# A convolution-attention hybrid on one core: two spreads of small vectors over channels go by way of DRAM instead of TensorE transposes

## The chip, the core and the metric

The kernel runs on 1 of the 8 cores of one Trainium2 chip. The metric is the device time of one execution in microseconds (us). The time before is 1663.79 us, the median of 3 runs (1658.05 to 1667.66). All profile figures come from one further execution that was recorded by the hardware profiler.

## What is computed

The input is four images of 32 channels, 128 x 128 float32. The reference has two layers; cut to what matters here:

```python
# layer 0: attention over channels' pixels, for each of 4 images b
q = pixel_unshuffle(x, 2).reshape(B, 128, 4096)        # 128 channels, 4096 positions
energy = einsum('bci,bcj->bij', q, q)                  # 4096 x 4096
d = sqrt(diagonal(energy))                             # norm of each position's vector
attn = softmax(energy / (d_i * d_j), axis=-1)
out = einsum('bcj,bij->bci', q, attn)
x = gamma * out + q                                    # back to image layout
# layer 1: tokens t = x as 8 x 8192 x 128
t = t + linear_attention(layernorm(t))                 # 8 heads
t = t + top2_of_8_experts(layernorm(t))
```

Two per-position vectors of layer 0 have to be multiplied into tiles whose rows are channels and whose columns are positions: `1/d` (the reciprocal norms, into the operand `qn` of the energy product), and `gamma / rowsum` (the reciprocal denominators of the softmax, into the attention output). Both vectors come about with positions on the partitions, because they are sums along the free dimension. So each must be turned and repeated over 64 rows ("spread") before the multiplication. The change concerns these two spreads alone.

## The kernel before

**Tiling.** The 4096 positions of an image are 8 chunks of 512 columns; one chunk is 4 blocks of 128. Only half of the symmetric energy matrix is computed. `attend` (L474) walks over chunk rows i = 0 to 7 and, in each, over jc = 0 to i: per 128 x 512 tile a matmul gives the energies (`pe`, L609), ScalarE takes the exponential (`pr`, L612), and a matmul adds its share to row i's output (`po`, L497). For jc < i the mirrored share is needed too: VectorE turns `pr` in 32 x 32 blocks into `F` (L421), `move` (L527) writes `F` to a DRAM tile `blocks` with one DMA (L530), and three steps later `bring` reads it back with the groups swapped in six DMAs (`swap_groups`, L545). These all go on SyncE's (SP's) queue. Some steps after that (`LAG = 57` units of an internal clock, L408) `transposed_share` (L429) uses `F` in four matmuls (`pg`, L433); VectorE then adds the result to `o[jc]` (L442). I call one passage of `F` through `blocks` a turn.

**Order.** The order of instructions on TensorE, VectorE, ScalarE and SP is the order in which the Python code issues them (`tc.manual_schedule`, L1413)[...]. Side jobs are generators. The list `timed` (L1414 on) has tuples (job, begin, end, count): the job is advanced by one `yield` whenever the image's progress, in per cent, asks for it, at a rate of count steps between begin and end. `steady` holds the closing work of each image (`layer1`), advanced once every `PACE = 10` clock units, and `stagger` (L166) passes each step on to several generators.

**First spread: `prep` (L348).** It prepares 2 chunks of an image (kc = 0 to 3; 16 calls in all with `prep_first`). It loads the pixels, turns them on VectorE into `qT`, squares and sums them (`squares`), and lets GpSimd (POOL) raise the sums to the power -1/2 (`pow_neg_half`, L163): `rn`, 128 x 8. VectorE then widens `rn` to `wide`, 128 x 4 x 2 x 64 (L388, two copies), four TensorE transposes against the identity put that into a PSUM bank `pnorm` (L399), and `scale` (L368) multiplies the pixels by it in four VectorE instructions (L372) into `qn`. `prep_first`, for the first two chunks, does this in another way (L344), which the change keeps.

**Second spread: `close_rows` (L731).** It closes two chunks of an image's output (kc = 0 to 3), once all mirrored shares are added (`missing()` is false). VectorE sums the denominators and takes reciprocals (L747, L748), widens them times gamma to `wide` (L752, two instructions), four TensorE transposes put that into a PSUM bank `pbd` (L774), and `divide` multiplies the output by it in four VectorE instructions (L761) into `df`. Then `df` is added to the tokens `T` (L783), their statistics follow, ScalarE normalises them (L696), and TensorE sums their Gram matrix (`pgram`, L728). For the last image `layer1` is split: the four `close_rows` run beside its attention, the rest after it (`last_parts`).

**Banks.** `hold` (L191) gives out one of three PSUM banks of the pool `ps_t` and makes sure that an earlier holder is emptied first; both spreads take a bank each time.

## Time and profile before

| quantity | value |
|---|---|
| time, median of 3 runs | 1663.79 us (1658.05 to 1667.66) |
| time of the profiled execution | 1659.2 us |
| its span, first to last instruction | 1657.4 us |
| mean granted clock of TensorE | 0.996 |
| TensorE (PE) busy | 1623.1 us, 98% of the span |
| VectorE (DVE) busy | 917.4 us, 55% |
| ScalarE (ACT) busy | 910.4 us, 55% |
| GpSimd (POOL) busy | 596.2 us, 36% |
| DMA | 332.81 MB in 241899 packets, mean 201 GB/s |

How to read it: a busy time is the union of an engine's instructions; TensorE's are pipelined, so one matmul's listed duration (mean ns) is longer than its slot in a row of matmuls, and the distance between two starts tells the slot. A float32 matmul of the program stands as two matmuls in the trace, a transpose as one. "Idle before" is the time in which an engine waited ahead of an instruction, with what ended the wait. SPq lines are the DMAs that SyncE's queue issues: their duration is the issue, not the transfer.

### The profile page before, as it was taken

The numbers are of one execution on the slowest core, as the hardware profiler recorded it, in microseconds if no ns is written. First come the engines' busy times: TensorE is split into PE (matmuls) and PEld (weight loads), VectorE is DVE, ScalarE is ACT, GpSimd is POOL, SyncE is SP. The second block draws the span as 40 slices with busy tenths as digits, with TensorE's granted clock in tenths as the row PEclk, the third lists the DMA queues.
The fourth block names the chain that finished last, engine by engine and source line by source line (L and its number), as shares of the span: only waits on it lengthen the run. The fifth ranks groups of instructions, "written<-read, shape, count | busy, mean of one in ns | idle before, by whom it ended". The sixth has DMA issues, their size and how long they took to land.

```text
span 1657.4 us, 21471 instructions
## 1 busy us (share of the span) xinstructions
PE 1623.1 (98%) x5288; PEld 856.9 (52%) x5288; DVE 917.4 (55%) x2359; ACT 910.4 (55%) x2863; POOL 596.2 (36%) x565
## 2 busy tenths in 40 slices
PE   8999999999999999999999999999999999999987
PEld 5444544455554455555564455555565445554643
DVE  4543353567486443559378453448559533344686
ACT  3555445566575555556575455556657455555376
POOL 1000000001014531456555543346546642436166
PEclk9999999999999999999999999999999999999999
DMA  4555656665349776986778868797668877885001
GB/s 147 199 181 174 198 186 213 230 212 170 131 171 277 246 220 213 271 249 176 207 200 254 265 208 255 214 287 200 167 196 239 277 222 246 240 254 168 15 14 39
DMA packets 241899, 332.81 MB, mean 201 GB/s; under 512 B 31984, under 2 KB 168304, under 8 KB 227440
## 3 DMA queue, kind: packets, MB, share of 16 engines
q1 hardware_dynamic: 207312, 291.92, 55.5%
q0 software_dynamic: 26624, 25.58, 7.5%
q10 hardware_dynamic: 7840, 13.93, 2.8%
q8 instruction: 45, 0.74, 0.2%
q14 instruction: 78, 0.64, 0.1%
HBM read 160.78 MB, written 175.80 MB: 203 GB/s over the span
## 4 chain that ended last, share of the span: by engine, by line
PE 84%; DMA 4%; DVE 4%; SPq 3%; ACT 2%; issue 2%; another core or an unknown queue 1%; POOL 0%; ACTq 0%; DVEq 0%; POOLq 0%
PE po L497 24%; PE pe L609 23%; PE pg L433 20%; PE pys L1117 3%; DMA blocks<-F 3%; PE py L1290 3%; PE pg L453 2%; SPq L545 2%; PE pat L854 2%; PE pys L1124 2%; PE pgram L728 1%; PE ptx L701 1%; DVE df L761 1%; PE pgv L839 0%
## 5 line engine op out<-in xcount | busy, mean ns | idle before, releaser
L612 ACT ACTIVATE pr<-pe 128x512 f32<-128x512 f32 (+1 forms) x576 | 322.4, 560 | 544.0 <-PE pe L609 448.2
L497 PE MATMUL po<-pr,qT 128*128 128x512 f32 (+3 forms) x1152 | 549.6, 559 | 4.2 <-ACT o L502 3.0
L609 PE MATMUL pe<-qn,qn 128*128 128x512 f32 x896 | 459.6, 595 | 2.6 <-ACT pr L612 1.6
L433 PE MATMUL pg<-F,qT 128*128 128x512 f32 x880 | 449.7, 592 | 1.1 <-DMA F<-blocks 1.1
L421 DVE STREAM_TRANSPOSE F<-pr 128x512 f32<-128x512 f32 x440 | 305.9, 702 | 144.8 <-ACT pr L612 127.0
L497 PEld LDWEIGHTS po<-pr,qT 128*128 128x128 f32 x1152 | 215.3, 190 | 251.7 <-issue 221.2
L1165 POOL DMA_INDIRECT acc<-ys,place x128 | 203.2, 1588 | 215.8 <-ACT pr L612 140.3
L438 ACT ACTIVATE junk<-F 128x512 bf16<-128x512 f32 x440 | 273.0, 620 | 1.2 <-DMA F<-blocks 1.2
L433 PEld LDWEIGHTS pg<-F,qT 128*128 128x128 f32 x880 | 166.7, 190 | 195.4 <-issue 181.0
L1053 POOL DMA_INDIRECT xs<-xn,place x192 | 186.0, 969 | 189.7 <-ACT pr L612 116.6
L609 PEld LDWEIGHTS pe<-qn,qn 128*128 128x128 f32 x896 | 155.0, 191 | 115.0 <-issue 104.6
L442 DVE TENSOR_TENSOR o<-o,pg 128x512 f32<-128x512 f32 x110 | 75.3, 684 | 207.9 <-PE pg L433 173.4
L1099 DVE TENSOR_TENSOR results<-pys,xn 128x256 f32<-128x256 f32 x120 | 49.9, 416 | 187.1 <-ACT xn L1093 122.0
L164 POOL TENSOR_TENSOR rn<-ss,neg_half 128x8 f32<-128x8 f32 (+1 forms) x17 | 27.2, 1602 | 320.9 <-DVE ss L296 320.8
L612 ACT ACTIVATION_READ_ACCUMULATOR pr<-pe 128x1 f32 x576 | 112.0, 194 | 0.0
L1093 ACT ACTIVATE xn<-pys 128x256 f32<-128x256 f32 x120 | 45.2, 377 | 112.5 <-PE pys L1124 94.5
L1117 PEld LDWEIGHTS pys<-ew_sb,xn 128*128 128x128 f32 x468 | 70.4, 191 | 53.0 <-issue 49.5
L1165 POOL DMA_INDIRECT yb<-ys,place x64 | 61.8, 965 | 84.5 <-DMA F<-blocks 31.1
L609 PE MATMUL pe<-qn 128*128 128x512 f32 (+3 forms) x256 | 90.2, 435 | 0.7 <-ACT qn L342 0.7
L438 ACT ACTIVATION_READ_ACCUMULATOR junk<-F 128x1 f32 x440 | 84.6, 192 | 0.0
L1117 PE MATMUL pys<-ew_sb,xn 128*128 x468 | 71.7, 275 | 0.4 <-ACT xn L1093 0.4
L164 POOL TENSOR_TENSOR rsa<-dm_a,neg_half 128x8 f32<-128x8 f32 x16 | 28.9, 1807 | 103.1 <-DVE sv_a L688 102.9
(216 smaller groups left out, 1521.1 us busy)
## 6 DMA issues: line engine op xcount, KB each, us to landing
blocks<-F SPq DMA_DIRECT2D x110, 1024.0 KB
F<-blocks SPq DMA_DIRECT2D x220, 192.0 KB
F<-blocks SPq DMA_DIRECT2D x220, 128.0 KB
xn<-xs SPq DMA_DIRECT2D x114, 132.0 KB
ys<-results SPq DMA_DIRECT2D x114, 128.0 KB
F<-blocks SPq DMA_DIRECT2D x220, 64.0 KB
below<-F SPq DMA_DIRECT2D x31, 384.0 KB
T<-in_x_dram SPq DMA_DIRECT2D x64, 128.0 KB
```

Of the source, the lines that this page charges most:

```text
L164: pinned(nc.gpsimd.tensor_tensor(dst, src, neg_half.to_broadcast(list(src.shape)), ALU.pow))
L421: f()
L433: nc.tensor.matmul(pg.rearrange("p (a f) -> p a f", a=4), st["qT"][i][:, ib, :], G[:, :, ib], start=(ib == 0), stop=(ib == NJ - 1),)
L438: nc.scalar.activation(junk, G[:, :, ib], AF.Copy, accum_out=st["sums"][:, NJ * i + ib, jc : jc + 1])
L442: nc.vector.tensor_tensor(st["o"][jc], st["o"][jc], pg, ALU.add)
L497: nc.tensor.matmul(row["po"][:, lo:hi], qT[blk // NJ][:, blk % NJ, :], w, start=start, stop=(row["left"] == 0))
L609: nc.tensor.matmul(pe[:, c0:], qn[jc][:, ts(j, P)], qn[i][:, c0:], start=True, stop=True)
L612: nc.scalar.activation(pr[:, c0:], pe[:, c0:], AF.Exp, accum_out=sums[:, t, i : i + 1]).ins
L1053: inst = nc.gpsimd.indirect_dma_start(xs[h], offset(place[:, i, k : k + 1]), xn[:, k, :], None)
L1099: nc.vector.tensor_tensor(result[:, :n], p[:, 2 * P : 2 * P + n * D].rearrange("p (j c) -> p j c", c=D), bufs[g % 6][:, :n, D : D + 1].to_ ...
L1117: nc.tensor.matmul(p[:, 2 * P + j * D : 2 * P + j * D + D], bufs[6 + g % 2][:, j, :D], weights[:, bass.ds(begins[2 * (g % 2) + j], D)], st ...
L1165: inst = nc.gpsimd.indirect_dma_start(to, None, ys, offset(place[:, i, k : k + 1]), compute_op=op)
```

## The change

In both spreads the widening on VectorE and the four transposes on TensorE go, for 14 of the 15 calls of `prep` (all but image 0, kc = 1) and for kc = 0, 1, 2 of `close_rows` in each image (kc = 3 stays as it was). In their place stands `spread_over_rows`:

- the vector is put into the first 8 columns of a 128 x 32 tile (`norms[0]` and `norms[1]` in turn for the norms, written by GpSimd directly; `norms[2]` for the denominators, times gamma in one VectorE instruction); the tiles are set to 1.0 once at the start;
- VectorE transposes it in 32 x 32 blocks into `turned`, so that each group of 32 partitions holds whole rows of positions;
- one step later SP writes `turned` to a DRAM tile of 128 x 32 (16 KB);
- five steps later SP reads it back in two DMAs, each to 64 partitions, every partition getting the same 4 pieces of 128 values (512 B); five steps later it is used.

The multiplications `scale` and `divide` read the result from SBUF, with another order of the columns (a, j, t for j, a, t), and are otherwise as before.

`close_rows` for kc < 3 now sums the denominators as soon as the image's last row of exponentials has passed its two chunks (`seen`) and the closing of kc - 2 has divided, ahead of the wait for the mirrored shares; after that wait it divides at once. It waits for kc - 1 to be added, and kc = 0 for the previous image's `sorted`, after the spread. `prep` for b + 1, kc = 3 is now advanced at 17 steps between 36% and 54% of the image (before: 38% to 62%), and the number of steps of a call of `prep` rises from 17 to 25 (image 0: from 16); what is left over runs on at the same rate. `place` has one buffer where it had two.

```diff
--- before.py
+++ after.py
@@ -318,6 +318,10 @@
                 xa[:, s, k].rearrange("p r (h t) e -> p (r h) e t", h=2),
             )
 
+    norms = [const.tile([P, S], F32, tag=f"norm{n}", name=f"norm_{n}") for n in range(3)]
+    for norm in norms:
+        nc.gpsimd.memset(norm, 1.0)
+
     def prep_first(st):
 
         b, kc = 0, 0
@@ -326,7 +330,7 @@
         qT = chunks_of(b, kc, st)
         yield
         ss = stat.tile([P, 2 * NJ], F32, tag="ss", name=f"ss_{b}_{kc}")
-        rn = stat.tile([P, 2 * NJ, 1], F32, tag="rn", name=f"rn_{b}_{kc}")
+        rn = norms[0][:, : 2 * NJ][:, :, None]
         for s in range(2):
             turn_quarters(s, xa, qT)
             squares(b, kc, s, qT, ss)
@@ -345,6 +349,25 @@
             done()
             yield
 
+    def spread_over_rows(norm, nm, tag, spread, gap):
+
+        turned = stat.tile([P, S], F32, tag="turned", name=f"turned_{nm}")
+        nc.vector.transpose(turned, norm)
+        yield
+        kept = dram.tile([P, S], F32, tag="norms", name=f"norms_{nm}", bufs=3)
+        nc.sync.dma_start(kept, turned)
+        for _ in range(gap):
+            yield
+        wide = work.tile([P, CH], F32, tag=tag, name=f"spread_{nm}", bufs=2)
+        for s in range(2):
+            nc.sync.dma_start(
+                wide[ts(s, 64)].rearrange("p (a f) -> p a f", a=4),
+                kept.rearrange("(a q) t -> a (q t)", q=S)[:, ts(s, P)].partition_broadcast(64),
+            )
+        spread.append(wide)
+        for _ in range(gap):
+            yield
+
     def prep(b, kc, st):
 
 
@@ -375,20 +398,27 @@
                     view(spread[own]),
                     ALU.mult,
                 )
-        rn = stat.tile([P, 2 * NJ, 1], F32, tag="rn", name=f"rn_{b}_{kc}")
+        on_chip = b == 0 and kc == 1
+        norm = norms[kc % 2]
         for s in range(2):
             squares(b, kc, s, qT, ss)
             if s == 1:
-                pow_neg_half(rn[:, :, 0], ss)
-            yield
-        for _ in range(ahead - 2):
-            yield
+                pow_neg_half(norm[:, : 2 * NJ], ss)
+            yield
+        if not on_chip:
+            yield from idle(1)
+            yield
+            spread = []
+            yield from spread_over_rows(norm, f"{b}_{kc}", "qs", spread, 5)
+            for s in range(2):
+                scale(s, spread[0], lambda ap: ap.rearrange("p (a j t) -> p a j t", a=4, t=S))
+            yield
+            return
+        rn = norm[:, : 2 * NJ][:, :, None]
         wide = work.tile([P, NJ, 2, 64], F32, tag="qs", name=f"wide_{b}_{kc}", bufs=2)
         for s in range(2):
             nc.vector.tensor_copy(wide[:, :, s], rn[:, ts(s, NJ)].to_broadcast([P, NJ, 64]))
         yield
-        if b:
-            yield
 
         def scale_all(bank):
             for s in range(2):
@@ -612,6 +642,8 @@
                         nc.scalar.activation(pr[:, c0:], pe[:, c0:], AF.Exp, accum_out=sums[:, t, i : i + 1]).ins
                     ]
                     own.append(pr)
+                    if i == NCH - 1 and j == NJ - 1:
+                        st.setdefault("seen", set()).add(jc)
                     if ending and jc == order[-1] and j == NJ - 1:
                         st["exps"] = True
                     after(2, partial(values, pr[:, c0:], t, c0, CH))
@@ -661,7 +693,7 @@
         lg = stat.tile([P, KT, E], F32, tag="lg", name=f"lg_{b}", bufs=1)
         first, second = (stat.tile([P, KT, E], F32, tag=nm, name=f"{nm}_{b}", bufs=1) for nm in ("first", "second"))
         weight = stat.tile([P, 2, KT, 1], F32, tag="weight", name=f"weight_{b}")
-        place = stat.tile([P, 2, KT], U32, tag="place", name=f"place_{b}")
+        place = stat.tile([P, 2, KT], U32, tag="place", name=f"place_{b}", bufs=1)
         begin = stat.tile([P, 2, NT + 1], U32, tag="begin", name=f"begin_{b}", bufs=1)
         turns = [[], []]
         gate = first
@@ -739,18 +771,31 @@
             late_rows = alone and kc >= 2
             last_rows = alone and kc == 3
 
-            while "exps" not in st if last_rows else missing():
-                yield from idle(1)
-            while b > 0 and kc == 0 and not states[b - 1].get("sorted"):
+            def summed():
+                return {2 * kc, 2 * kc + 1} <= st.get("seen", set()) and (kc < 2 or kc - 2 in st["divided"])
+
+            for flag in ("divided", "added"):
+                st.setdefault(flag, set())
+            far = kc < 3
+            while not summed() if far else "exps" not in st if last_rows else missing():
                 yield from idle(1)
             den, rd = (stat.tile([P, 2 * NJ], F32, tag=nm, name=f"{nm}_{b}_{kc}") for nm in ("den", "rd"))
             nc.vector.tensor_reduce(den, st["sums"][:, ts(kc, 2 * NJ), :], AX.X, ALU.add)
             nc.vector.reciprocal(rd, den)
-            wide = work.tile([P, NJ, 2, 64], F32, tag="grp", name=f"rdx_{b}_{kc}", bufs=2)
-            for s in range(2):
-                one = rd[:, ts(s, NJ)][:, :, None]
-                nc.vector.tensor_scalar(wide[:, :, s], one.to_broadcast([P, NJ, 64]), gam, None, ALU.mult)
+            if far:
+                norm = norms[2]
+                nc.vector.tensor_scalar(norm[:, : 2 * NJ], rd, gam, None, ALU.mult)
+                spread = []
+                yield from spread_over_rows(norm, f"den_{b}_{kc}", "grp", spread, 5)
+            else:
+                wide = work.tile([P, NJ, 2, 64], F32, tag="grp", name=f"rdx_{b}_{kc}", bufs=2)
+                for s in range(2):
+                    one = rd[:, ts(s, NJ)][:, :, None]
+                    nc.vector.tensor_scalar(wide[:, :, s], one.to_broadcast([P, NJ, 64]), gam, None, ALU.mult)
+            while far and missing() or not (kc - 1 in st["added"] if kc else b == 0 or states[b - 1].get("sorted")):
+                yield from idle(1)
             df = work.tile([P, 8, HW2, 2], F32, tag="df", name=f"df_{b}_{kc}", bufs=1)
+            spread_view = "p (a j t) -> p a j t" if far else "p (j a t) -> p a j t"
 
             def divide(pb):
                 for s in range(2):
@@ -761,26 +806,32 @@
                         nc.vector.tensor_tensor(
                             df[own].rearrange("p (a k) (h t) r -> p r a (k h) t", a=4, h=2)[:, r2],
                             o[rows].rearrange("p (a j t) -> p a j t", a=4, t=S),
-                            pb[own].rearrange("p (j a t) -> p a j t", a=4, t=S),
+                            pb[own].rearrange(spread_view, a=4, t=S),
                             ALU.mult,
                         )
 
-            yield
-            if not last_rows:
-                yield
-                yield
-            pb, done = hold(f"pbd_{b}_{kc}", divide)
-            for j in range(NJ):
-                nc.tensor.transpose(pb[:, ts(j, P)], wide[:, j].rearrange("p s c -> p (s c)"), ident)
-            yield
+            if not far:
+                yield
+                if not last_rows:
+                    yield
+                    yield
+                pb, done = hold(f"pbd_{b}_{kc}", divide)
+                for j in range(NJ):
+                    nc.tensor.transpose(pb[:, ts(j, P)], wide[:, j].rearrange("p s c -> p (s c)"), ident)
+                yield
             while missing():
                 yield from idle(1)
-            done()
+            if far:
+                divide(spread[0])
+            else:
+                done()
+            st["divided"].add(kc)
             if not late_rows:
                 yield
                 yield
             tk = T[:, ts(kc, 8), :]
             nc.vector.tensor_tensor(tk, tk, df.rearrange("p k w r -> p k (w r)"), ALU.add)
+            st["added"].add(kc)
             bs, stats = batch_stats("a", 8 * kc, 8)
             for j in range(8):
                 stats[j]()
@@ -1451,7 +1502,7 @@
         timed = []
         if b + 1 < B:
             timed.append((prep(b + 1, 2, nxt), 0.5, 16, 17))
-            timed.append((prep(b + 1, 3, nxt), 38, 62, 17))
+            timed.append((prep(b + 1, 3, nxt), 36, 54, 17))
     for steps, _ in steady:
         for _ in steps:
             pass
```

## The prediction

> **What bounds the kernel now.** I read the page's busy times and slices first, then the busy time by stage, then what TensorE waited for.
>
> ```profile
> PE 1623.1 (98%) x5288; PEld 856.9 (52%) x5288; DVE 917.4 (55%) x2359; ACT 910.4 (55%) x2863; POOL 596.2 (36%) x565
> ...
> PE   8999999999999999999999999999999999999987
> ...
> DMA  4555656665349776986778868797668877885001
> ```
>
> TensorE is at work everywhere but at the two ends; no other engine comes near. DMA engines are two thirds busy, more in the slices where experts' rows are moved. By stretches of 41 or 42 us (busy us of PE, PEld, DVE, ACT, POOL, then clock, DMA share, GB/s):
>
> ```profile
> 580.00:621.00 41.00, 41.00 (x149) 22.54 (x148) 17.64 (x32) 21.13 (x67) 16.52 (x19) 1.00 0.70 217
> ...
> 1326.00:1367.00 41.00, 39.41 (x126) 19.97 (x125) 13.13 (x27) 21.93 (x70) 19.67 (x22) 1.00 0.71 219
> ...
> 1492.00:1533.00 41.00, 37.58 (x117) 19.09 (x116) 19.13 (x45) 21.14 (x68) 27.50 (x29) 0.97 0.57 167
> 1533.00:1574.00 41.00, 37.35 (x197) 27.30 (x196) 27.99 (x90) 15.68 (x41) 6.25 (x7) 0.95 0.07 16
> ```
>
> Of 34.3 us of idle TensorE, 6.4 lie in the first 41 us and 20.0 after 1492 us; the 1450 us between have 7.9. There the time is the sum of TensorE's slots, and a slot taken out is a slot gained, unless a new wait fills it. TensorE's waits (total us, times, longest):
>
> ```profile
> PE pnorm L399 <- DVE wide L388: 2.8, 2, 2.5
> PE ptd L523 <- ACT gd L513: 2.4, 1, 2.4
> ...
> PE pg L433 <- DMA F<-blocks: 1.1, 1, 1.1
> ```
>
> The pnorm wait is nearly all that of image 0, kc = 1, which the change keeps. The mirrored shares waited once for a DMA.
>
> [...]here whole landings take longer (the chain shows 2.8 to 3.4 us for F<-blocks).
>
> **Removed.** Rows by form (count | busy us, mean ns | idle before):
>
> ```profile
> L752 DVE TENSOR_SCALAR rdx<-rd,gam 128x256 f32<-128x256 f32 x32 | 10.3, 364 | 0.6
> L774 PE MATMUL pbd<-ident,rdx 128*128 128x128 f32 x64 | 9.6, 273 | 0.1
> ...
> L399 PE MATMUL pnorm<-ident,wide 128*128 128x128 f32 x60 | 9.5, 283 | 2.8 <-DVE wide L388 2.8
> ...
> L388 DVE COPY wide<-rn 128x256 f32<-128x256 f32 x30 | 7.9, 304 | 1.1 <-POOL rn L164 1.1
> ```
>
> The slot of a set of four is seen in TensorE's timeline (start, us, what):
>
> ```profile
> 331.84 0.60 PE L774 MATMUL pbd<-ident,rdx 128*128 128x128 f32 x4
> 332.28 1.02 PE L609 MATMUL pe<-qn,qn 128*128 128x512 f32 x2
> ```
>
> From the set's first start to the next matmul's: 0.44 us. I looked at all 31 sets: 0.44 in 26 and 0.46 to 0.49 in 4 more, the first apart (0.78, with its wait). 56 pnorm transposes (14 sets) and 48 pbd transposes (12 sets) go: 26 x 0.44 = **11.4 us**, all on a TensorE without gaps. VectorE loses 28 x 0.304 + 24 x 0.364 = 17.2 us.
>
> **Added on engines.** VectorE gets 26 transposes of 128 x 32 and 12 small multiplications. A transpose of 128 x 128 takes 283 ns and of 128 x 256 412 ns in this trace, so about 0.19 us by the slope (estimate): 4.9 us, and 12 x 0.17 = 2.0. So VectorE has 10 us less. `scale` and `divide` stay the same: 682 to 687 ns with a PSUM operand, 681 ns for the sum of two SBUF tiles of 512 columns (L1200). VectorE is 45% idle: nothing on the path. Three memsets fall into POOL's wait from 2.2 to 8.4 us. Nothing: 0.
>
> **Added on SP and the DMAs.** 26 x 3 = 78 DMAs join some 1000 on SP. Six F<-blocks issue in 2.7 us, so a spread costs about 1.3 us of SP. Its 640 packets, at the 71 ns that a q1 packet takes now (55.5% of 16 engines x 1657 us over 207312), are 2.8 us of all 16 engines, 74 us in all: 4.5% more of a load of 66%. This matters only where `F` is late already. I paired each turn's six issues with its first pg matmul: of 141 turns the issue ends 5 to 28 us before use, mostly 10 to 17. Eleven have 7.5 us or less (rows 5 to 7 of the first image, row 2 of the last two, row 7 of the last). The tightest but one, in SP's timeline:
>
> ```profile
> 1495.89 6.61 SPq L545 DMA_DIRECT2D F<-blocks  x6
> 1502.60 0.37 SPq L530 DMA_DIRECT2D blocks<-F  x1
> ```
>
> and its use in TensorE's:
>
> ```profile
> 1507.52 1.02 PE L433 MATMUL pg<-F,qT 128*128 128x512 f32 x2
> ```
>
> The issue ends at 1502.5, use is at 1507.5, and landing takes 3 to 4 us: a margin of about 1. In the order of the built instructions some eight of these eleven have a spread's DMAs within the turns before them. Each pays from 0 to about 1.3 us (SP's time), so 0 to 10 us together. Below nothing is excluded here; the timing of `prep` 3 moves four pixel loads away from the token loads that crowd SP before 1326 us (1.6 us idle there), worth at most that. I take **+2.5 us**.
>
> **Moved.** The built order of TensorE is the same but for the removed sets, `pgram` groups some rows earlier, and the tail. `qn` is ready 19 or more matmuls ahead of its first use (in the tightest case, image 0's chunk 4: 42 before), some 16 us; no loss. The spreads of denominators start while `missing()` still holds. On the new waits: SP waits for VectorE's `turned` one step after its issue, with turns queued behind; VectorE waits for the spread five steps after the reads. A step of `close_rows` is 10 clock units of about 0.25 us (an image is 1568 units in some 388 us), so 12 us stand against a landing of 3 to 4 us; in `prep` more. POOL's power was waited for before too, at the same distance. Cost 0; without that cover see the slow rival.
>
> In the tail (last image), kc = 2 closes earlier, so more `pgram` and `ptx` lie before the last po instead of in the gaps after 1547 us. But o[6]'s sum waits in front of kc = 2's statistics on VectorE, and the last po now stands behind kc = 2's first pgram, which needs those statistics. Walking both orders through with the slots above, the last `divide` ends within 0.5 us of where it did without the stalls at 1526 to 1534 us, and PE's later part, with its 36 spare transposes of 5.0 us, begins up to 3 us sooner. Between -4 and +3; I take **-1**.
>
> **Sum.** -11.4 + 2.5 - 1 = -9.9 us on the profiled execution's 1659.2 us: 1649.3, a ratio of 0.9940. That execution stands 4.6 us under the median shown, so 1663.8 x 0.9940 = **1653.8 us**.
>
> **Rivals.**
> - *The late F eats the gain.* For it: margins of 1 us, and SP as the issuer of all turns. Against: a single DMA wait of 1.1 us today. At 8 to 10 us of waits and no gain in the tail, 1663.8 - 11.4 + 9 = about 1661.
> - *Slower: VectorE stands still at spreads.* VectorE waits in order for a read that sits in SP's queue behind blocked DMAs; behind it wait the block transposes for `F`, so later turns start late too. It decides from SP being over 8 us behind (12 us less 4 us of landing). Single waits of SP now reach 9.6 us ahead of a turn and 13.4 us ahead of the last stores, so it can be reached, but seldom. If it happened at 20 of 26 spreads, each holding TensorE by 1.1 us: +22 - 11.4 gives about 1674.
> - *More than the slots.* If the stalls of 4 us at 1526 to 1534 us go with the new order, 1653.8 - 5 gives about 1648.
> - That the transposes are not removed can't be: the built order lacks them. That another engine becomes the bound: VectorE and ScalarE are at 55%.
>
> **Chances.** Slots gained with little loss (1648 to 1659) 0.60; late F (about 1661) 0.27; more than the slots 0.06; slower 0.07. The range takes the first three with the bounds of F and tail: 1646 to 1665. A measurement can tell about 0.5% (8.3 us) from no change: under 1655.5 is faster. That has most of the first case and the third: 0.60; slower by over 0.5% is the slow case alone, 0.07; the rest, 0.33, within.
>
> **What would show it.** PE busy falls by 11 to 16 us (sets overlap in the union); PE's idle time between 41 and 1492 us stays under 12 us. PE's waits for F<-blocks show the loss: up to 4 us as predicted, 8 or more for the first rival. VectorE's waits for spread on its `scale` and `divide` rows should be near 0; tens of us there speak for the slow rival. The prediction is wrong if TensorE's idle time grows by more than 5 us in the middle, or if the tail after 1492 us changes by more than 4 us.

## The result and the profile after

| | before | after |
|---|---|---|
| median | 1663.91 us, 6 runs, 1658.05 to 1667.66 | **1683.88 us**, 6 runs, 1681.23 to 1691.76 |
| ratio, 95% interval | | **1.0132** (1.0102 to 1.0161) |
| profiled execution, its span | 1659.2, 1657.4 us | 1683.45, 1681.7 us |
| mean granted clock | 0.996 | 0.993 |
| PE idle between 41 and 1492 us | 7.5 us | 27.8 us |

The changed kernel is 1.3% slower; 0.6% faster was forecast. (Below, each experiment's ratio is to the kernel before in the same set of runs; in the third and fifth set that kernel ran at 1651 us and in the others at 1660 to 1664, for a reason that no profile here shows, so ratios of these two sets are not laid beside the others'.)

The page after, the engines' rows as shown of before:

```profile
PE 1624.8 (97%) x5184; PEld 849.0 (50%) x5184; DVE 908.5 (54%) x2345; ACT 912.3 (54%) x2863; POOL 599.2 (36%) x568
...
PE   8999999989999999999999999999999899998897
```

TensorE runs 104 instructions fewer (5288 to 5184), so the transposes are gone, and yet it is busy 1.7 us longer: what remained got slower. There are eights in the middle now, where there were none. The same four stretches by the clock (columns as before: busy us of PE, PEld, DVE, ACT, POOL, then clock, DMA share, GB/s):

```profile
580.00:621.00 41.00, 41.00 (x146) 22.23 (x145) 16.34 (x30) 21.37 (x66) 17.52 (x19) 1.00 0.79 239
1326.00:1367.00 41.00, 36.55 (x89) 16.46 (x88) 13.88 (x23) 17.81 (x57) 25.05 (x27) 0.96 0.70 214
1492.00:1533.00 41.00, 36.93 (x96) 16.61 (x94) 20.02 (x44) 18.86 (x60) 15.00 (x15) 0.99 0.83 245
1533.00:1574.00 41.00, 39.18 (x133) 21.83 (x133) 20.77 (x58) 21.97 (x69) 25.43 (x24) 0.93 0.36 91
```

The first is as full as before. The second has lost 2.9 us of TensorE's time and shows a clock of 0.96, with nothing of the tail in it yet. TensorE's waits (total us, times, longest):

```profile
PE pgram L760 <- ACT xn L728: 13.6, 7, 3.3
PE pys L1175 <- DMA xn<-xs: 7.0, 8, 2.0
PE pe L639 <- ACT pr L642: 6.2, 2, 4.4
PE pg L463 <- DMA F<-blocks: 4.8, 3, 2.7
```

The forecast looked for `F`, which is last here and near its size (4.8 us; up to 4 said). The first two rows are new. In the rows by form (count | busy us, mean ns | idle before) `pgram` was, before,

```profile
L728 PE MATMUL pgram<-xn 128*128 128x128 f32 x256 | 34.1, 277 | 0.5 <-ACT xn L696 0.5
```

and is, after, with the two multiplications that read the spreads:

```profile
L760 PE MATMUL pgram<-xn 128*128 128x128 f32 x256 | 42.8, 307 | 13.8 <-ACT xn L728 13.6
...
L806 DVE TENSOR_TENSOR df<-o,spread_den 64x512 f32<-64x512 f32 x48 | 32.9, 685 | 8.8 <-DMA ys<-results 5.7 <-DMA spread_den<-norms_den 2.2
L395 DVE TENSOR_TENSOR qn<-xx,spread 64x512 f32<-64x512 f32 x48 | 32.7, 682 | 13.1 <-DMA spread<-norms 12.6
```

256 Gram matmuls wait 13.8 us and take 8.7 us more. VectorE stands 12.6 us for the norms' spreads, but only 2.2 us for those of the denominators; `df` waits 5.7 us for something the forecast never named, a store `ys<-results`.

**Where the time comes in.** The 1152 `pe` matmuls of the attention are the same in all kernels, so the start of the k-th one is a milestone. Differences to before in the profiled execution, between milestones; "image's end" is from 24 `pe` matmuls ahead of it to 48 after it, where the closings stand:

| us against before | up to image 0's end | end 0 | end 1 | end 2 | `pe` 1008 to 1032 | `pe` 1130 on | all |
|---|---|---|---|---|---|---|---|
| after | -2.8 | +4.2 | +8.6 | +10.3 | +3.4 | +3.1 | +24.2 |
| `norms_timing` | -3.7 | -1.0 | -0.5 | -0.5 | -1.8 | +2.8 | -3.0 |
| `order_only` | -0.2 | +3.2 | +3.6 | +3.4 | -1.0 | -1.0 | +8.6 |
| `order_only_b` (the same kernel) | +0.8 | +3.3 | +6.8 | +3.4 | -0.8 | -2.2 | +13.6 |
| `order_dmas` | +1.4 | +4.7 | +8.8 | +8.5 | -3.1 | -0.7 | +19.7 |
| `dens_only` | +1.1 | +6.0 | +8.2 | +6.9 | -1.0 | +0.4 | +21.0 |
| `dens_later` | -0.1 | +6.4 | +3.0 | +2.5 | -0.7 | +6.7 | +16.7 |
| `divide_later` | -2.8 | +4.8 | +4.3 | +7.3 | +3.0 | +5.6 | +18.4 |
| `own_dens` | +0.4 | +6.0 | +3.5 | +2.3 | -2.4 | +0.1 | +9.1 |
| `own_after` | -1.7 | +4.9 | +5.1 | +6.7 | 0.0 | +1.7 | +16.6 |
| `own_after_kc1` | -1.3 | +4.0 | +1.8 | +1.8 | -3.1 | -1.8 | +5.2 |

(The rows are the experiments below; stretches left out make up the sum. Each row is one execution. Executions of the kernel before lie up to 8 us from their median, so a total is no sharper than that. A stretch is sharper, but not always: the two executions of one kernel, `order_only` and `order_only_b`, agree within 0.2 us at two ends and differ by 3.2 us at the third.) Between the ends, where nothing waits, the changed kernel gains what was forecast: from `pe` 400 to 552 it is 1.31 us ahead, three sets of 0.44. At each end of an image it loses 4 to 10 us.

### The profile page after: what moved, and what is told of

Read it like the earlier page. It is cut to its first block, busy times and chain, and to the rows that moved or that the text cites. A ratio compares the mean times of both kernels' runs of the same rounds, so it can differ in the third digit from the quotient of the medians.

```text
span 1681.7 us, 21331 instructions
## 1 busy us (share of the span) xinstructions
PE 1624.8 (97%) x5184; PEld 849.0 (50%) x5184; DVE 908.5 (54%) x2345; ACT 912.3 (54%) x2863; POOL 599.2 (36%) x568
## 4 chain that ended last, share of the span: by engine, by line
PE 81%; DMA 6%; DVE 5%; ACT 2%; issue 2%; SPq 2%; POOL 2%; another core or an unknown queue 0%; ACTq 0%; DVEq 0%; POOLq 0%
PE po L527 24%; PE pe L639 23%; PE pg L463 19%; PE pys L1168 3%; PE py L1341 3%; PE pg L483 2%; PE pgram L760 2%; DMA xn<-xs 2%; PE pat L905 2%; PE pys L1175 1%; DVE df L806 1%; POOL yb L1216 1%; DMA F<-blocks 1%; PE ptx L733 1%; SPq L575 1%
## 5 line engine op out<-in xcount | busy, mean ns | idle before, releaser
L164 POOL TENSOR_TENSOR norm<-ss,neg_half 128x8 f32<-128x8 f32 (+1 forms) x17 | 27.3, 1604 | 338.1 <-DVE ss L296 338.0
```

What stands on the lines that cost most here:

```text
L164: pinned(nc.gpsimd.tensor_tensor(dst, src, neg_half.to_broadcast(list(src.shape)), ALU.pow))
```

## The experiments

The theories that the expectations name with letters were these. A: VectorE, standing still at the norms' spreads, holds up what is queued behind it. B: the changed order of the closings brings TensorE to `pgram` before ScalarE's `xn` is there. C: the three DMAs of each spread make SP's queue, and with it other transfers, late. D came last and says which transfer: the stores `ys<-results`. An edit is shown against the changed kernel, if nothing else is said.

### One part alone

`norms_only` has the closings as they were, and `prep` as changed. `dens_only` has `prep` as it was, at 38 to 62%, and the closings as changed.

> The norms go through DRAM as in the changed kernel; the denominators are turned by TensorE as before. Theory A (the last steps of the next image's chunk 1 are all drawn at once at an image's end, so VectorE stands for the landing of its spread there): three waits of VectorE of 4 us on qn's rows stay, and most of the loss with them: 14 sets x 0.44 = 6 us gained, 12 to 15 us lost, so 1670 to 1674. Theory B (the closings' divide now comes four steps earlier before pgram's neighbours, and TensorE reaches pgram before ScalarE's xn): the loss goes with the denominators, so 1658 to 1661, TensorE's waits for xn back to 0.5 us. Theory C (SP's queue is late for everything behind a spread): loss in proportion to DMAs, 42 of 78, so about 1674.

> The denominators go through DRAM as in the changed kernel; the norms are turned by TensorE as before, and the timing of the preparation is the one before. Theory A: no wait of VectorE at the image's ends, so 12 sets x 0.44 = 5 us gained and little lost: 1659 to 1662. Theory B: TensorE's waits for xn (13.6 us in 7) stay, so 1670 to 1674. Theory C: in proportion to DMAs, 36 of 78, so about 1673.

Measured: `norms_only` 1661.37 us, ratio 0.999 (0.9977 to 1.0003); `dens_only` 1681.03, 1.0109 (1.0091 to 1.0128). The loss is, for the most part, in the denominators, and larger than any theory said for `dens_only` (1674 at most). `dens_only` has none of the norms' spreads, and has 15.1 us of `pgram` waits in 6: so A, if it costs anything, can't be the main cause. `norms_only` also has `place` with one buffer, so that part of the change is not the cause either.

### Giving the norms' steps time; dividing later

```diff
 prep_in_time:
-            timed.append((prep(b + 1, 1, nxt), 80, 99, 17))
+            timed.append((prep(b + 1, 1, nxt), 80, 99, 25))
 divide_later:
             if far:
+                for _ in range(4):
+                    yield
                 divide(spread[0])
```

> The changed kernel with one number changed: the next image's chunk 1 gets 25 steps in its stretch, as many as it has now, where it had 17. Theory A: VectorE's three waits of 4 us for the spread go (under 1 us left), the ends of images 0 to 2 give back 4 us each, so 1670 to 1673. Theory B: TensorE's waits for xn stay at 13 us, the time at 1681 to 1685. Theory C: SP is as late, 1681 to 1685.

> The changed kernel with four steps put back between the last share of a closing and its divide, as before. Theory B: TensorE's waits for xn fall from 13.6 us to under 3 us, so 1670 to 1674. Theory A and C: under 3 us of change, 1681 to 1685.

Measured: `prep_in_time` 1697.3 us, 1.0207 (1.0182 to 1.0232), `divide_later` 1681.25, 1.0124 (1.01 to 1.0148). The first missed badly: its VectorE still stood 14.4 us at `qn`, up to 9.4 us in one go, so more steps did not give the reads time, and image 0's end alone is 12.9 us longer than before, for 4.2. As a test of A it decides nothing; it shows that the number of steps isn't harmless. `divide_later` moved the waits more than the time. TensorE's waits of `pgram` for `xn` fell from 13.6 us in 7 to 3.4 in 1; none is left at the ends of images 0 to 2, and ends 1 and 2 cost 4.3 and 7.3 us for 8.6 and 10.3. But in the last image `pgram` waits 7.6 us for 5.8, 4.1 of them for `xnT`, and the stretch from `pe` 1130 on costs 5.6 us for 3.1; the median can't be told from the changed kernel's (the intervals overlap).

### The order without the transfers

`order_only` keeps the changed order of the closings, but spreads the denominators on TensorE as before, right ahead of the division, with eleven empty steps where the spread's steps were, and has the norms as before: no DMA is added. `order_only_b` is the same kernel once more.

```diff
             if far:
-                divide(spread[0])
-            else:
-                done()
+                pb, done = hold(f"pbd_{b}_{kc}", divide)
+                for j in range(NJ):
+                    nc.tensor.transpose(pb[:, ts(j, P)], wide[:, j].rearrange("p s c -> p (s c)"), ident)
+            done()
```

> Denominators turned by TensorE again and norms as before the change, no new DMA at all, but the closings keep the changed kernel's order: the same steps, the same conditions, pgram at the same places of TensorE's program (2 to 4 pe matmuls nearer to its statistics than before). Theory B (the new order of the closings lets TensorE reach pgram before ScalarE's xn): the loss stays, TensorE's waits for xn are 10 us or more and the time is 1676 to 1686. Theory C (the new DMAs make SP and the DMA engines late): nothing is added, so the time is that of before, 1661 to 1664.

> The same kernel as order_only, on this chip, to stand beside the other three: 1.004 to 1.006. If its ratio is 1.009 or more here, the ratio of these kernels to the one before depends on the chip, and only kernels of one call may be compared closely.

Measured: 1669.56 us, ratio **1.0048** (1.0032 to 1.0064), and 1669.96, 1.005 (1.0032 to 1.0069). No transfer is added and no transpose removed: the new order alone costs 8 us. That is less than theory B said (1676 to 1686, with waits for `xn` of 10 us or more; they are 5.1 us in 5), so the order is a part of the loss. The timeline (start, us, what) at the end of image 1, with SP's last store of the results and VectorE's first division ahead of TensorE's Gram matmuls, before:

```profile
735.61 0.39 SPq L1103 DMA_DIRECT2D ys<-results  x1
...
739.22 2.78 DVE L761 TENSOR_TENSOR df<-o,pbd 64x512 f32<-64x512 f32 x4 [0.48 <-PE pbd L774]
...
757.66 1.05 PE L728 MATMUL pgram<-xn 128*128 128x128 f32 x8
...
761.12 1.95 PE L728 MATMUL pgram<-xn 128*128 128x128 f32 x16
```

and in `order_only`:

```profile
739.44 0.39 SPq L1144 DMA_DIRECT2D ys<-results  x1
...
741.22 2.79 DVE L795 TENSOR_TENSOR df<-o,pbd 64x512 f32<-64x512 f32 x4 [1.07 <-DMA ys<-results]
...
756.34 1.64 PE L753 MATMUL pgram<-xn 128*128 128x128 f32 x8
...
761.10 3.18 PE L753 MATMUL pgram<-xn 128*128 128x128 f32 x16 [0.74 <-ACT xn L721]
```

Eight matmuls take 1.64 us for 1.05, sixteen 3.18 for 1.95. They stand two to four of the program's `pe` matmuls (four to eight of the trace's) earlier than before: the first behind the 293rd for the 295th, a later group behind the 300th for the 304th. So they come directly behind the activations that make their `xn`, and TensorE follows ScalarE row by row: ScalarE makes its four rows in 1.65 us, and the eight matmuls, two for each row, take 1.64. From the first division to the first `pgram` there are 15.1 us, where before there were 18.4. The 3.3 us between were slack of the chain division, addition to `T`, statistics, POOL's power, ScalarE's `xn`, `pgram`, and the new order took them away.

### The transfers without use, and with one more step

`order_dmas` is `order_only` with the 12 spreads' 36 DMAs beside it; what they read back goes to a DRAM tile that nobody reads (in the change it goes to SBUF). `order_spaced` and `order_spaced_b` are `order_only` with one step more between normalising and Gram matmuls, in both halves; `dens_later` is `dens_only` with four steps ahead of the division, `dens_spaced` that with the extra step too; `after_timing` is the changed kernel with `prep` at 38 to 62% again.

```diff
 order_dmas, against order_only:
-            for _ in range(11 if far else 0):
-                yield
+            if far:
+                norm = norms[2]
+                nc.vector.tensor_scalar(norm[:, : 2 * NJ], rd, gam, None, ALU.mult)
+                yield from spread_over_rows(norm, f"den_{b}_{kc}", "grp", [], 5)
 order_spaced, in both halves of close_rows' end:
+            yield
 after_timing:
-            timed.append((prep(b + 1, 3, nxt), 36, 54, 17))
+            timed.append((prep(b + 1, 3, nxt), 38, 62, 17))
```

> The kernel with the changed order of closings alone, TensorE still turning the denominators, with the 12 spreads' 36 DMAs put in besides: the write as in the change, the two reads into DRAM memory that nothing reads. It is over that order alone (1669.6) by what the DMAs cost by their place in SP's queue and on the DMA engines, no consumer waiting. Theory C: 8 to 14 us more, 1677 to 1684, with TensorE's wait for F<-blocks near 340 us back. If the cost is VectorE waiting for the landing, 1668 to 1672.

> The kernel with the changed order of closings alone (no new DMA), with one more step between ScalarE's normalise and TensorE's pgram on the same rows. If the loss of that order (8 us) is pgram following ScalarE row by row (eight pgram matmuls take 1.64 us instead of 1.05, and the waits for xn), it goes: 1660 to 1664 beside 1662 of the kernel before. If it is something else in the order (VectorE's and GpSimd's queues), it stays: 1667 to 1671.

> The same kernel as order_spaced, on another chip. By its trace (5.6 us over the kernel before, where the order alone has 8.6) the ratio is 1.003 to 1.004: one step more between normalise and pgram takes back a third. If the ratio is 1.008 or more again, it does not help and the trace was a good execution.

> Denominators through DRAM, norms as before the change, and four steps put back between the last share of a closing and its divide. Theory B: the waits for xn go, 12 sets x 0.44 = 5.3 us stay gained, 1658 to 1663. Theory C: 36 DMAs remain, so 1672 to 1681.

> Denominators through DRAM, norms as before the change, four steps ahead of divide and one more step between normalise and pgram. If row-by-row pgram is 7 us of what was left with four steps (1674.6), 1666 to 1669; if what is left is the DMAs' alone, 1673 to 1676.

> The changed kernel with the timing of the fourth chunk's preparation put back to 38, 62. With norms alone that gave 4 us (1661.4 to 1657.6). If it is the same thing here: 1679 to 1681, and no stall near 1341 us. If the denominators' waits cover it: 1683 to 1685.

| | median | ratio (95%) | set |
|---|---|---|---|
| `dens_later` | 1674.62 | 1.0083 (1.0058 to 1.0109) | 2 |
| `order_dmas` | 1677.89 | 1.0164 (1.015 to 1.0178) | 3 |
| `order_spaced` | 1664.89 | 1.0094 (1.0077 to 1.011) | 3 |
| `dens_spaced` | 1691.34 | 1.0249 (1.0235 to 1.0263) | 3 |
| `after_timing` | 1674.61 | 1.0142 (1.0127 to 1.0158) | 3 |
| `order_spaced_b` | 1668.29 | 1.0103 (1.0087 to 1.012) | 5 |

**Transfers that nobody waits for bring the loss back.** `order_dmas` came out where theory C put it (1677 to 1684): 8 us over `order_only` by the medians, which are of different sets, and 6 to 11 us by the spans of the profiled executions. TensorE waits 13.7 us for `xn` in 7 (`order_only`: 5.1 in 5, `dens_only`: 15.1 in 6), and at images' ends 1 and 2 it loses 5.2 and 5.1 us more than `order_only`, 2.0 and 5.1 more than `order_only_b`. The same place in its timeline:

```profile
742.68 0.39 SPq L1146 DMA_DIRECT2D ys<-results  x1
...
748.07 2.79 DVE L797 TENSOR_TENSOR df<-o,pbd 64x512 f32<-64x512 f32 x4 [4.84 <-DMA F<-blocks]
...
763.55 2.07 PE L753 MATMUL pgram<-xn 128*128 128x128 f32 x8 [4.12 <-ACT xn L721]
```

VectorE's division stands 4.84 us. The trace names `F<-blocks`, but in the program this division waits for no `F`; it waits for three stores `ys<-results` of the previous image. The last of them is issued at 742.68, and the division starts 5.4 us after that. In `order_only`, whose trace names the store, it starts 1.8 us after it (739.44 to 741.22). That the longer wait is for the store too is read from the program here; the runs with another buffer (below) bear it out. `df` and `results` have the same buffer:

```python
keep["results"] = work.tile([P, 4, 2, D], F32, tag="df", name=f"results_{b}", bufs=1)
df = work.tile([P, 8, HW2, 2], F32, tag="df", name=f"df_{b}_{kc}", bufs=1)
```

15.5 us after the division began come the Gram matmuls, after a wait of 4.1 us. In the changed kernel:

```profile
740.84 0.40 SPq L1154 DMA_DIRECT2D ys<-results  x1
...
743.75 2.82 DVE L806 TENSOR_TENSOR df<-o,spread_den 64x512 f32<-64x512 f32 x4 [2.26 <-DMA ys<-results]
...
758.79 1.64 PE L760 MATMUL pgram<-xn 128*128 128x128 f32 x8 [1.98 <-ACT xn L728]
```

There the store is issued 5.2 us later than before (735.61) with TensorE only 0.1 us behind at milestone 552, and the division starts 2.9 us after it. By the records of landings in the two traces the store has landed 2.8 us after its issue here (at 743.67, just ahead of the division), and 1.8 us after it in the kernel before (at 737.37). Why a store lands sooner or later isn't shown; DMA engines were busy 0.79 of 709 to 801 us in `order_dmas`, 0.76 in `order_only`.

**One step more helps the row, not the time.** `order_spaced` has no `pgram` wait at image 0's end (+0.9 us there for +3.2), and its Gram matmuls take 34.4 us in all, as before (34.1), but it has waits of 1.7 and 2.3 us at the other two ends and pauses elsewhere. Two sets of runs give no gain over `order_only`: by the criterion on record (1.008 or more) the step does not help. How much that says stays open, as the kernel before stood at 1651 in both sets. That the order's 8 us come from the lost slack is therefore read from the traces; no run that gives slack back shows it in the time. `dens_later` is 0.26% better than `dens_only`, with intervals that overlap a little. Its four steps take the `pgram` waits from the ends of images 0 to 2, and ends 1 and 2 cost 3.0 and 2.5 us for 8.2 and 6.9; but in the last image, where the statistics stood behind POOL's gathers, `pgram` waits 8.1 us and the last stretch costs 6.7 us for 0.4. `dens_spaced` is worse than all that was expected. `after_timing` keeps the ends' loss (+4.4, +8.9 and +10.4 us), so the changed time of `prep` is not its cause; but the stand at `pe` 1010, which the changed kernel has near 1341 us, is gone there.

### The shared buffer

D: if the store matters because of the buffer, `results` in a tile of its own must take the loss back. For images 0 and 1, `results` goes to the tag "wide", which is idle then:

```diff
-                keep["results"] = work.tile([P, 4, 2, D], F32, tag="df", name=f"results_{b}", bufs=1)
+                tag, n = ("wide", 2) if b < B - 2 else ("df", 1)
+                keep["results"] = work.tile([P, 4, 2, D], F32, tag=tag, name=f"results_{b}", bufs=n)
```

`own_before` is the kernel before with that edit, `own_dens` is `dens_only` with it, `own_after` the changed kernel with it and `prep` at 38 to 62%.

> The kernel before with the same other buffer for the results. Its divide does not wait for the stores in the trace, so every theory expects no change: 0.998 to 1.002.

> Denominators through DRAM, norms as before the change, and the results of images 0 and 1 in a buffer of their own, so that divide no longer waits for their stores. Theory D (the loss at the ends of images 1 and 2 is divide waiting for the last store of results behind other DMAs): TensorE's waits for xn at those two ends fall from 9 us to 3 or less, the two ends cost 4 us each where they cost 8.2 and 6.9, and the ratio falls from 1.011 to 1.006. If the DMAs hold TensorE in another way, the ratio stays at 1.009 to 1.012.

> The changed kernel with the old timing of the fourth chunk (38, 62) and the results in a buffer of their own. Theory D: 1.004 to 1.007 where the changed kernel has 1.013. If the DMAs hold TensorE in another way (late F, late loads of xn): 1.010 to 1.013.

Measured: `own_before` 1660.95 us, 1.0007 (0.9996 to 1.0017); `own_dens` 1669.53, **1.0063** (1.004 to 1.0086); `own_after` 1676.34, 1.0097 (1.0072 to 1.0122), just short of the range for the other ways (1.010 to 1.013) and outside D's (1.004 to 1.007). With both parts in, the buffer takes back 3.8 us at end 1 and 3.7 at end 2 (`after_timing`, which differs in the buffer alone, has +8.9 and +10.4 there), and most of the loss stays. The buffer is worth nothing to the kernel before, and 0.46% (7.6 us) to `dens_only`, as D said. The ends of images 1 and 2, where the edit applies, go from +8.2 and +6.9 to +3.5 and +2.3; image 0's end, which has no earlier `results`, stays at +6.0. The waits of `pgram` at ends 1 and 2 go from 8.5 us to 2.4. In `dens_only` the division waits for the store (again under the name `F<-blocks`):

```profile
744.82 0.39 SPq L1147 DMA_DIRECT2D ys<-results  x1
...
748.98 2.81 DVE L799 TENSOR_TENSOR df<-o,spread_den 64x512 f32<-64x512 f32 x4 [3.75 <-DMA F<-blocks]
...
763.88 2.08 PE L753 MATMUL pgram<-xn 128*128 128x128 f32 x8 [3.33 <-ACT xn L721]
```

In `own_dens` it doesn't wait:

```profile
744.04 0.39 SPq L1147 DMA_DIRECT2D ys<-results  x1
744.62 2.80 DVE L799 TENSOR_TENSOR df<-o,spread_den 64x512 f32<-64x512 f32 x4
...
759.86 1.28 PE L753 MATMUL pgram<-xn 128*128 128x128 f32 x8
...
764.25 3.18 PE L753 MATMUL pgram<-xn 128*128 128x128 f32 x16 [1.17 <-ACT xn L721]
```

The store is issued as late as in `dens_only`, the division starts 0.6 us after its issue, and the first group waits for nothing. What is left is the tight order again (3.18 us for sixteen).

### The norms' DMAs at images' ends; the other queue; the best version

`own_after_kc1` is `own_after` with chunk 1's norms spread by TensorE in every image, since these steps lie at an image's end. `both_act` is `divide_later` with the spreads' three DMAs on ScalarE's queue. `norms_timing` is `norms_only` with the old time of `prep`.

```diff
 own_after_kc1:
-        on_chip = b == 0 and kc == 1
+        on_chip = kc == 1
 both_act:
-        nc.sync.dma_start(kept, turned)
+        nc.scalar.dma_start(kept, turned)
...
-            nc.sync.dma_start(
+            nc.scalar.dma_start(
```

> own_after, with the norms of chunk 1 of each image, whose preparation lies at the end of the image before, turned by TensorE again (three sets more of 0.44 us, nine DMAs fewer). If those DMAs stand ahead of the loads of xn in SP's queue and make them late, TensorE's wait for xn<-xs falls from 8.5 us to under 4, and the ratio from 1.0097 to 1.005 to 1.007. If the denominators' DMAs do it, the wait stays at 7 to 9 us and the ratio at 1.009 to 1.011.

> The changed kernel with four steps put back ahead of divide, and the spread's three DMAs issued by ScalarE's queue, not by SP's. If SP's order is what makes xn's loads and F late there (TensorE waited 6.2 us for xn<-xs and 4.0 us for F<-blocks with the same steps and SP's queue), both waits fall under 3 us together: 1670 to 1675. If the DMA engines' load is what makes them late, they stay: 1679 to 1684. If ScalarE's wait for VectorE's turned tile holds its activations, TensorE's waits for pr grow instead: over 1684.

> Norms through DRAM, denominators as before, and the timing of the fourth chunk's preparation put back to what it was before the change (38, 62 for 36, 54). If the stall of 4.4 us at 1316 us in the profile with norms alone comes from where that preparation now lies, it goes, and the gain of 14 sets x 0.44 = 6.2 us shows: 1655 to 1659. If it comes from the norms' DMAs as such, it stays: 1660 to 1663.

**Both parts together.** `own_after_kc1` took 1670.83 us, 1.0129 (1.011 to 1.0149). TensorE's waits for the loads of tokens, in `own_after`:

```profile
PE pys L1175 <- DMA xn<-xs: 8.5, 9, 2.8
```

and in `own_after_kc1`:

```profile
PE pys L1175 <- DMA xn<-xs: 1.3, 3, 0.6
```

The trace did as expected: the waits go, the ends of images 1 and 2 fall to +1.8 us each, and the profiled execution's span is 11.4 us shorter (it was the fastest of its four). The ratio did not come to what was expected; the kernel before stood at 1651 us in that set, so the gain is shown by the trace and the raw median (5.5 us less than `own_after`), not by a ratio. Two things went at once, so which of them delays the loads stays open: SP's spread DMAs just ahead of them (`spread<-norms` takes 2.1 us of SP at 715.80 in `own_after`, the next load goes out at 720.16), or VectorE's stand of 3.7 to 4.7 us at `qn`, behind which `results` stand. Neither can be all of it. At the ends of images 1 and 2 these loads make TensorE wait 6.1 us in the changed kernel, 0.6 in `dens_only` and not at all in `norms_only`, so it takes both parts. But in `dens_spaced`, with other steps and without any DMA for norms, they still make it wait 3.9 us there, and in `both_act`, where VectorE stands 0.5 us at `qn` and SP issues no spread, 3.3.

**The other queue** is worse: `both_act` took 1701.85 us, 1.0237 (1.0221 to 1.0254), with 14.2 us of waits for `F` in 7 (`divide_later`: 4.0 in 2) and 6.3 for the loads of tokens in 7 (6.2 in 6). None of the three expectations holds: neither wait fell, and TensorE's waits for `pr` did not grow. Nothing is gained by ScalarE's queue in this run; where its loss comes from is not shown.

**Norms alone, at the old time**: `norms_timing` took 1657.56 us, **0.9974** (0.9959 to 0.999), and beats both kernels. It gains 4.3 us of the 6.2 that 14 sets of 0.44 promise; at `pe` 1008 it is 5.6 us ahead. `norms_only` differs from it in the time of `prep` 3, and loses 4.3 us in one place near 1316 us (`pe` 1010). TensorE's waits put it down to nothing that the profile shows ("issue"):

```profile
PE pe L639 <- issue: 4.3, 1, 4.3
```

The changed kernel stands 4.4 us at the same place in its program (1341 us). With the old time of `prep` the stand is gone in both (`norms_timing`, `after_timing`), so that time brings it on; what it is that waits there stays open.

## Why the prediction was wrong

- **Removed: right.** 104 transposes went, at 0.44 us a set wherever nothing waits (1.31 us for three sets between images' ends). VectorE's transposes of 128 x 32 took 184 and 211 ns for 0.19 us said, its 12 small multiplications 243 ns each for 0.17.
- **Moved: the first failed step.** The prediction saw that the order was "the same but for the removed sets, `pgram` groups some rows earlier", and gave that no price. It costs 8 us (`order_only`, twice). As the traces have it, the few rows were the slack of the longest chain at an image's end: 3.3 us of 18.4. In the profile before, `pgram` has no wait but one of 0.5 us, so this slack isn't visible in waits, only in the 18.4 us from division to Gram matmul.
- **SP and DMAs: the second failed step.** The term was +2.5 us (0 to 10) and priced one consumer only, late `F`, which came out at 4.8 us of waits against up to 4 said (the largest, 2.7 us, at image 0's end, where nearly every kernel with the denominators' DMAs has one of 1.3 to 3.0). The way that cost more was not looked at: the stores `ys<-results` come later (at image 1's end the last is issued 5.2 us later than before and lands 6.3 us later), the division shares their buffer, and statistics, `xn` and `pgram` follow. 36 unread DMAs add about 8 us to `order_only`; the buffer is worth 7.6 us to `dens_only`. With the norms' DMAs beside them the loads of tokens are late too (7.0 us of waits). Three inputs of the term were low as well: SP had 1541 DMAs to issue, not some 1000, a spread takes 1.8 us of SP on average, not 1.3, and about 688 packets, not 640 (q1 had 17888 more for 26 spreads).
- **New waits at cost 0: the cover was wrong, the price is open.** VectorE's waits were to be near 0; at `qn` they are 12.6 us in 3. There the steps of chunk 1 that are left over do not go on at the same rate: they are run off at once at an image's end, without the clock between them ("in `prep` more" does not hold there). That alone is not enough, as with norms alone the same steps wait 1.6 to 2.7 us. This is the place of the slower rival, at 3 spreads for its 20; what these stands cost was not separated from SP's DMAs.
- **The slower rival** had 0.07. It asked for 20 stands of VectorE and priced them as lost turns; the loss came mostly by a chain that it didn't name. The rival of the late `F` was near in its size of waits and wrong in what it left out.
- **What some waits drag behind them was not in the sum**: half clock (last section), by estimate 5.1 us.
- **The tail**: -1 forecast; from `pe` 1130 on it is 3.1 us longer.
- **Its own signs of being wrong came**: TensorE's idle time between 41 and 1492 us is 27.8 us, for under 12 said (before it was 7.5; the prediction's 7.9 has 0.4 us of the very end in it), and its busy time rose by 1.7 us where it was to fall by 11 to 16.

The sum in the profiled execution: -11.4 (slots) + 8.6 (`order_only`) + 11.1 (`order_dmas` over it) + 7.0 (loads) + 4.4 (the stand at 1341) = +19.7 of +24.2. This is a rough account: the terms are single executions (with `order_only_b` the split would be 13.6 and 6.1), and the last two are waits, put in as if nothing else covered them. The 4.5 us left are within what two executions differ by, and no run assigns them. PE's busy time adds up in the same rough way: -11.4, +8.7 for `pgram`, +5.1 for the clock give +2.4; +1.7 was measured.

## What to carry to other kernels

Where a kernel has no idle time, look at distances, not only at waits: before moving anything, measure from a chain's first instruction to its consumer in the bound engine's program, and count each step that the change takes out of it. Here DMAs that nobody read cost 8 us, and the buffer of a store beside such DMAs was worth 7.6. So when DMAs join a shared queue, count as touched also what the other transfers of that queue release, reused buffers among it: follow each tag with one buffer to its last reader, a store included. And take the parts of a change one by one: here one half gains 0.26%, the other loses 1.1%.

## What the hardware showed that was not expected

With some short waits TensorE's clock fell to half for some time. In the changed kernel, by stretches:

```profile
1150.00:1156.80 6.80, 3.76 (x15) 2.14 (x14) 6.49 (x31) 2.01 (x5) 3.23 (x3) 1.00 0.45 150
1156.80:1160.20 3.40, 3.40 (x8) 1.50 (x6) 1.37 (x6) 2.21 (x8) 3.07 (x3) 0.50 0.52 150
```

The columns are as above. In the first lies a `pgram` wait of 3.04 us; in the second the clock is 0.50, and matmuls of 512 columns start 0.85 us apart instead of 0.43 (the trace lists 0.60 us for one, on average). The clock record has such stretches, of 3.41 us or twice that, from 1156.8, 1341.1, 1532.2, 1586.8 and 1607.3 us, 20.5 us together apart from the very end; before, from 21.4, 1530.1 and 1557.4 us, 10.2 us. So 10.2 us more at a clock of 0.50, which by estimate lost half of that, about 5.1 us. The five starts lie whole multiples of 3.41 us apart (54, 56, 16 and 6), and the three of before too (442 and 8). The length of a wait alone does not decide. At the first four starts stand waits of 3.04, 4.40, 3.30 and 2.52 us: the first and the last of these ended 1.4 and 0.5 us ahead of the half clock (at 1155.3 and 1586.4), the other two 0.4 and 0.8 us after it had begun (at 1341.5 and 1533.0). A wait of 2.71 us for `F` (to 338.8) was not followed by it: the clock is 1.00 from there to 342.3 us. The wait that ends at 21.3 us before and at 21.4 us in the changed kernel is of 2.48 and 2.54 us; the clock in the 3.4 us behind it is 0.51 before and 1.00 in the changed kernel. The stretch from 1607.3 us follows several waits, none over 0.7 us. What decides is not shown. In these two traces a wait thus cost itself, and where a stretch of half clock came with it, by estimate 1.7 us more for each 3.41 us of it.
